# A block-matching convolution pipeline on one core: the first image's load and first strips, and the last image's transfers, put in another order and on other queues

## The chip, the cores and the metric

The kernel runs on one core of one Trainium2 chip. The time is the device time of one execution in microseconds (us); the figure for a kernel is the median of its runs. A profile was taken of one execution as well: it lists every instruction of the five engines (PE for matrix products, DVE, ACT, POOL, and SP, which only issues transfers) and the packets of the DMA queues.

## The reference, cut to what matters

The input is eight images of 32 channels and 128 x 128 pixels in f32. Two layers, each with a residual sum, are applied to them; each begins with a normalisation over groups of two channels of an image.

```python
# layer 0, on the normalised image x
for dy in range(-2, 3):
    for dx in range(-2, 3):
        sh = shifted copy of x (clipped at the edge)
        cost = 3x3 box sum of ((x - sh) ** 2).sum(channels)
idx = the 8 cheapest of the 25 offsets, for every pixel
g   = the 8 shifted copies that idx names          # 32 * 8 = 256 channels
h   = relu   (depthwise3x3(conv1x1(g, w1), w2))
h   = relu   (depthwise3x3(conv1x1(h, w3), w4))
h   = sigmoid(depthwise3x3(conv1x1(h, w5), w6))
y   = agg(inverse_dct(h * dct(g)));  x1 = x_in + y
# layer 1, on the normalised x1
out = x1 + conv(x1, one 5x5 kernel for every channel, padding 2)
```

## The kernel before, in words

**Steps.** An image is cut into 16 strips of 8 rows, with one more step after them for the rows that lag behind. The main loop (L1015) goes over all strips of all images, and in each step it works on three strips at once: stage 3 of strip s-2, stage 2 of strip s-1, stage 1 of strip s, then the end of strip s-2 (`for i in (3, 2, 1, 0)`, L1026). A stage is a 1x1 product (`pv` L641 and `p` L665), and a depthwise 3x3, half of it on DVE (`acc`, L692 to L699) and half on PE (`pw`, L718).

**Units.** The strip that enters next is gathered in four units, a half strip of four rows and half of the eight copies each. A unit has a load (`gather_load`: POOL fetches the pixels `xt`, L559/L565, and the indices `ib`, L574), a selection (`gather_select`: ACT turns indices into 0/1 masks `sel`, L588/L589), and the gathering itself (`gather_pixels`: PE multiplies pixels with masks, `pg` L603, and ACT copies the result to `xb`, L610). One unit is gathered in each part of a step.

**Preparation.** Before strips of an image can be gathered, its best offsets must be known. `prep` loads the image in four row groups of 32 rows with three rows around each (L84, and L89 for edge rows), takes statistics (L348), normalises (L359), then for six bands of rows subtracts shifted copies (`df`, DVE L413), squares them (ACT L421) and sums over channels (`pd`, PE L428). `costs` sums patches (`v`, L477 to L489; its input comes over two transfers through memory, L443 and L461/L468), transposes (`ct` L494/L498) and picks the eight cheapest offsets (DVE L505/L506, 32 pairs of instructions per row and group); `places` turns them into indices (`oc` L520 to L529, `pi` L538, `li` L540, stored by L541). This is done in four chunks of 8 rows in each of the four row groups, so strip n needs chunk n % 4, and the strips 0 to 3 need all four chunks.

**What sets the order.** PE, DVE and ACT execute in the order in which the program is written (`manual_schedule`, L999); POOL and SP are ordered by a scheduler. Preparation is cut into tasks that wait in queues D (DVE work, with a cost), A, P and Q. `tick` (L984) lets so much D work into each part of a step as the image's share asks for; `until` (L991) runs tasks until a condition holds; `push` takes a third value, a number of turns to wait. The 36 pairs of squares have cost `PAIR` = 1.95 and come first, in the order of the queue. A `unit` load first calls `until` the chunk that it needs is ready (L967 to L969), with everything written in between.

**The head.** The setup (L147 to L189) loads the depthwise weights (L122, L153), the three 1x1 weights (L173) and the dct weights (32 small transfers, L283) on the SP queue; the 1x1 weights are transposed on PE (L188) and copied by ACT (L189). The first image comes over the ACT queue alone. The loop L1005 loads units 0 to 6, for which chunk 1 must be ready, and gathers units 0 to 3. Then the steps begin.

**The tail.** Layer 1 of the last image runs after the last step. `load` (L840) reads four times 8 channels (L852, L854, L857), DVE normalises (L864), PE forms the 5x5 product by bands (L891), DVE adds it (L903) and the result goes out: for each group of 8 channels two halves e = 0, 1 of four channels, each in two transfers of the rows 0 to 61 and 66 to 127 (L905). The four rows between are computed apart (`middle`, L926 to L939, out at L948). All of these transfers are issued by POOL.

Of the kernel before, what the change touches and what calls it, by code (L numbers as in the profile page):

```python
# [19 lines left out]
R = 8  # L20
# [22 lines left out]
def bm3d_conv_preact(  # L43
# [33 lines left out]
    def load_image(b, engine):  # L77

        xn = xnp.tile([P, HR, HX], F32, name=f"xn_{b}", tag="xn")
        for rg in range(4):  # L80
            s = slice(C * rg, C * (rg + 1))
            lo = 32 * rg - 3
            a, z = max(lo, 0), min(lo + HR, H)
            engine.dma_start(xn[s, a - lo : z - lo, 2 : 2 + W], x[b, :, a:z, :])  # L84
            for r in range(HR):
                y = lo + r
                if y < 0 or y >= H:
                    y = min(max(y, 0), H - 1)
                    engine.dma_start(  # L89
                        xn[s, r : r + 1, 2 : 2 + W], x[b, :, y : y + 1, :]  # L90
                    )
        return xn

    first = load_image(0, nc.scalar)
# [52 lines left out]
    with tc.tile_pool(name="setup", bufs=1) as sp, tc.tile_pool(  # L147
        name="setup_ps", bufs=2, space=bass.MemoryType.PSUM
    ) as spp:
        dwt = sp.tile([P, 3, 4, 9], F32, name="dwt")  # L150
        for n, w in enumerate((w2, w4, w6)):
            for g in range(4):
                nc.sync.dma_start(  # L153
                    dwt[C * g : C * (g + 1), n],
                    w[:P].rearrange("(q c) o a b -> c q (o a b)", c=C),
                )
            nc.gpsimd.memset(dwd[0:C, n, 1], 0.0)
            for u in range(2):
                for dy in range(3):
                    s = slice(C * (u + dy), C * (u + dy + 1))  # L160
                    nc.gpsimd.tensor_tensor(
                        dwd[s, n, u],
                        cst[s, C_M32 : C_M32 + C]
                        .unsqueeze(1)
                        .unsqueeze(1)
                        .to_broadcast([C, 4, 3, C]),
                        dwt[s, n, :, 3 * dy : 3 * dy + 3].unsqueeze(3).to_broadcast([C, 4, 3, C]),
                        ALU.mult,
                    )
        wide = {}  # L170
        for name, w in (("w1", w1), ("w3", w3), ("w5", w5)):
            t = sp.tile([P, 2, CK], F32, name=f"nat_{name}", tag=f"nat_{name}")
            nc.sync.dma_start(t, w.rearrange("(m p) i a b -> p m (i a b)", p=P))  # L173
            if name == "w1":

                nat, t = t, sp.tile([P, 2, CK], F32, name="w1_kc")
                for m in range(2):
                    nc.vector.tensor_copy(
                        t[:, m].rearrange("p (k c) -> p k c", c=C),
                        nat[:, m].rearrange("p (c k) -> p k c", k=K),  # L180
                    )
            wide[name] = t
        for name, dst in (("w1", lw1), ("w3", lw3), ("w5", lw5)):
            for g in range(2):
                ps = spp.tile([P, CK], F32, name=f"ps_{name}_{g}", tag="ps")
                for m in range(2):
                    src = wide[name][:, m, g * P : (g + 1) * P]
                    nc.tensor.transpose(ps[:, m * P : (m + 1) * P], src, ident)  # L188
                nc.scalar.copy(dst[:, g], ps)  # L189
# [32 lines left out]
    def run(which, credit=1e9):  # L222

        q, took = queues[which], 0.0
        for _ in range(len(q) if which != "D" else 1000):
# [8 lines left out]
            )  # L234
            if i is None or took >= credit:
                break
# [37 lines left out]

    def mixes():
# [9 lines left out]
        yield "D", 1.0  # L285
# [529 lines left out]
    def layer1(b):  # L815
# [17 lines left out]
        last = b == NB - 1  # L833
        if last:
# [5 lines left out]
        def load(c):  # L840
# [11 lines left out]
            nc.gpsimd.dma_start(t[0], src[:, c : c + 4])  # L852
            for h in range(2):
                nc.gpsimd.dma_start(  # L854
                    t[1][64 * h : 64 * h + 64], src[64 - 64 * h : P - 64 * h, c + 4 : c + 8]
                )
            nc.gpsimd.dma_start(t[2], src[:, c + 4 : c + 8])  # L857
# [18 lines left out]
        for c in range(0, C, 8):  # L876
# [24 lines left out]
            for e in range(2):  # L901
                y = t[2 * e]
                nc.vector.tensor_add(y, y, ps[e])  # L903
                for a, z in ((0, 62), (66, P)):
                    nc.gpsimd.dma_start(  # L905
# [84 lines left out]

    def until(cond, credit):  # L991
        while not cond():
            now[0] += 1
            run("D", credit)
            run("A")
            run("P")
            run("Q")

    with tc.manual_schedule(engines=ORDERED):  # L999
        push(prep(0))  # L1000
        push(mixes())
# [3 lines left out]
        for u in range(7):  # L1005
            unit(gather_load, u)
            unit(gather_select, u - 2)
            unit(gather_pixels, u - 3)
        u = 4
# [5 lines left out]
        for s in range(len(steps) + 2):  # L1015
            if s < len(steps):
# [6 lines left out]
                if n == NS - 1 and b + 1 < NB:  # L1023
                    until(lambda: b + 1 in ready, 4.0)
                    xbd[b + 1] = dram.tile([P, 2, H, W], F32, name=f"xbd_{b+1}", tag="xbd")
            for i in (3, 2, 1, 0):  # L1026
# [21 lines left out]
                run("Q")  # L1048
                if s < len(steps):
                    unit(gather_select, u + 1, (0,))  # L1050
                    unit(gather_load, u + 3)
# [6 lines left out]
                if s < len(steps):  # L1058
# [4 lines left out]
                if s < len(steps):  # L1063
                    unit(gather_select, u + 1, (1,))
                    u += 1
                next(dt, None)
# [71 lines left out]
```

## Time and profile before

| | us |
|---|---|
| median of 4 runs | 6864.76 |
| the runs | 6874.87, 6871.53, 6846.25, 6857.99 |
| the profiled execution, own time | 6841.15 |
| its span, first to last instruction | 6839.4 |

| engine | busy, us | share of the span |
|---|---|---|
| PE | 6359.8 | 93% |
| DVE | 5856.3 | 86% |
| ACT | 5064.6 | 74% |
| POOL | 3241.2 | 47% |

| place in the span, us | what |
|---|---|
| 40.75 | statistics of the first image begin (L348) |
| 52.78 | first `df` (L413) |
| 137.66, 182.0, 230.19, 266.28 | indices of chunks 0 to 3 stored (L541) |
| 231.61, 271.45, 314.33, 357.15 | first product of strips 0 to 3 (L641) |
| 6779.56 | last rows of x1 of the last image have landed |
| 6796.21 | first result transfer issued (L905) |

The profile's page gives busy times for the whole span, the span in 40 slices, the DMA queues, the chain of work that ended last, and the costliest groups of instructions. Windows give the same busy times for chosen stretches; a timeline lists an engine's instructions with the idle time before them and what ended it. The view of DMA gives, for 40 slices of a stretch, the tenths of the time that the 16 engines were busy, and what each queue moved.

### The profile page before, as it was taken

How to read it: one execution, taken by the hardware profiler on the slowest of the kernel's cores; microseconds unless marked ns; L12 is line 12 of the kernel's file. 1: busy time of each engine (PE TensorE's matmuls, PEld its weight loads, DVE VectorE, ACT ScalarE, POOL GpSimd, SP SyncE). 2: the span in 40 equal slices, each digit the busy share in tenths (PEclk: the TensorE clock that was granted, in tenths of full speed). 3: DMA queues.
4: the chain of work that ended last, by engine and by line, in shares of the span. 5: the costliest groups of instructions: out<-in, count | busy, mean ns of one | idle time of the engine just before them, and what ended most of it. 6: DMA issues, size and time to landing. Idle time of an engine off the chain costs nothing.

```text
span 6839.4 us, 232443 instructions
## 1 busy us (share of the span) xinstructions
PE 6359.8 (93%) x101090; PEld 2969.0 (43%) x101090; DVE 5856.3 (86%) x8822; ACT 5064.6 (74%) x6698; POOL 3241.2 (47%) x5351
## 2 busy tenths in 40 slices
PE   4699899999999999999999999999999999999997
PEld 1344444444444444444444444444444444444443
DVE  6799988988888898888989888899888999877776
ACT  4687768777787777977778777787768777686772
POOL 6345436544464443644446444464435543344334
PEclk8899999999999999999999999999999999999998
DMA  3556656666566675665756657566565666566553
GB/s 80 135 150 149 155 135 159 162 147 161 148 154 156 150 162 142 165 148 146 171 130 163 161 144 168 133 169 155 149 153 150 166 157 147 139 163 159 149 151 82
DMA packets 809531, 1019.84 MB, mean 149 GB/s; under 512 B 255456, under 2 KB 619936, under 8 KB 808512
## 3 DMA queue, kind: packets, MB, share of 16 engines
q0 software_dynamic: 422432, 745.61, 42.5%
q1 hardware_dynamic: 381056, 256.86, 17.0%
q8 instruction: 796, 13.04, 0.8%
q10 hardware_dynamic: 5024, 2.49, 0.2%
q14 instruction: 223, 1.83, 0.1%
HBM read 553.25 MB, written 217.01 MB: 113 GB/s over the span
## 4 chain that ended last, share of the span: by engine, by line
PE 46%; DVE 14%; DMA 8%; ACT 6%; issue 5%; POOL 3%; SPq 0%; POOLq 0%; ACTq 0%; DVEq 0%
PE pw L718 16%; PE pv L641 11%; DVE acc L695 10%; PE p L665 10%; DMA t<-t 4%; PE pg L603 3%; PE p L891 2%; PE pc L777 2%; ACT ib L588 1%; PE pa L798 1%; PE pd L428 1%; ACT df L421 1%; DVE acc L785 1%; DMA ib<-idxd 1%; ACT acc L692 1%
## 5 line engine op out<-in xcount | busy, mean ns | idle before, releaser
L695 DVE SCALAR_TENSOR_TENSOR acc<-tv,dwv,acc 128x1024 f32<-128x1024 f32 (+3 forms) x3264 | 4032.3, 1237 | 255.3 <-ACT acc L692 139.0
L718 PE MATMUL pw<-t,dwd 96*32 96x508 f32 (+6 forms) x19392 | 2154.3, 591 | 125.2 <-DMA t<-t 101.3
L574 POOL DMA_DIRECT2D ib<-idxd x1024 | 569.8, 558 | 1827.3 <-ACT sel L589 1663.6
L718 PEld LDWEIGHTS pw<-t,dwd 96*32 96x32 f32 (+1 forms) x19392 | 712.6, 112 | 1248.2 <-issue 1153.9
L588 ACT ACTIVATE ib<-ib,nplace 128x1024 bf16<-128x1024 bf16 x1024 | 1170.2, 1143 | 18.5 <-DMA ib<-idxd 18.5
L589 ACT ACTIVATE sel<-ib 128x1024 f32<-128x1024 bf16 x1024 | 1084.7, 1059 | 32.5
L665 PE MATMUL p<-acc,lw 128*32 128x256 f32 x16768 | 994.0, 382 | 23.2 <-ACT tv L649 22.7
L641 PE MATMUL pv<-acc,lw 128*128 128x512 f32 (+1 forms) x2112 | 970.9, 601 | 28.6 <-DVE acc L785 20.0
L758 POOL DMA_DIRECT2D xf<-xbd x1088 | 651.5, 632 | 307.4 <-PE pc L777 80.9
L665 PEld LDWEIGHTS p<-acc,lw 128*32 128x32 f32 x16768 | 557.5, 111 | 452.8 <-ACT tv L649 62.4
L649 ACT COPY tv<-pv 128x512 f32<-128x512 f32 (+2 forms) x784 | 439.0, 577 | 400.7 <-PE pv L641 389.5
L603 PEld LDWEIGHTS pg<-sel,xt 128*32 128x32 f32 x45056 | 577.4, 111 | 265.8 <-ACT sel L589 66.4
L421 ACT ACTIVATE df<-df 128x786 f32<-128x786 f32 (+2 forms) x576 | 468.4, 859 | 297.1 <-DVE df L413 294.2
L603 PE MATMUL pg<-sel,xt 128*32 128x48 f32 x45056 | 595.5, 207 | 94.8 <-ACT sel L589 57.9
L731 ACT ACTIVATE acc<-pw 128x512 f32<-128x512 f32 (+2 forms) x808 | 441.6, 572 | 286.4 <-PE pw L718 286.0
L641 PEld LDWEIGHTS pv<-acc,lw 128*128 128x128 f32 x2112 | 379.3, 190 | 521.7 <-issue 399.1
L413 DVE TENSOR_TENSOR df<-xn 128x786 f32<-128x786 f32 (+2 forms) x576 | 527.5, 966 | 82.6 <-PE pd L428 81.8
L699 ACT ACTIVATE acc<-acc 128x1024 f32<-128x1024 f32 (+3 forms) x408 | 416.8, 1022 | 227.3 <-DVE acc L695 227.1
L672 ACT COPY t<-p 128x512 f32<-128x512 f32 x800 | 424.1, 570 | 128.0 <-PE p L665 125.9
L692 ACT ACTIVATE acc<-tv,dwv 128x1024 f32<-128x1024 f32 (+3 forms) x408 | 454.6, 1114 | 57.7 <-PE pa L798 39.8
L641 PE MATMUL pv<-xb,lw 128*128 128x512 f32 x1024 | 474.9, 606 | 0.0
L665 PE MATMUL p<-xb,lw 128*32 128x256 f32 x8192 | 467.7, 380 | 0.2 <-DVE xy L903 0.2
(151 smaller groups left out, 5774.8 us busy)
## 6 DMA issues: line engine op xcount, KB each, us to landing
ib<-idxd POOLq DMA_DIRECT2D x1024, 256.0 KB, 4.5
xbd<-xb POOLq DMA_DIRECT2D x128, 1024.0 KB, 7.0
xf<-xbd POOLq DMA_DIRECT2D x960, 128.0 KB, 7.0
t<-t SPq DMA_DIRECT2D x792, 128.0 KB
t<-t SPq DMA_DIRECT2D x384, 256.0 KB
tv<-tv SPq DMA_DIRECT2D x384, 130.0 KB
xt<-xtd POOLq DMA_DIRECT2D x240, 176.0 KB, 4.6
xl<-xs POOLq DMA_DIRECT2D x256, 64.0 KB, 2.7
```

The costliest lines, as they stand in the source:

```text
L413: nc.vector.tensor_sub(df[:, :, ca:cz], xn[:, r0 : r0 + SR, ca:cz], xn[:, r0 + dy : r0 + dy + SR, ca + dx : cz + dx],)
L421: nc.scalar.activation(df[:, :, ca:cz], df[:, :, ca:cz], AF.Square)
L574: nc.gpsimd.dma_start(ib.rearrange("p k y x -> p (k y x)"), idxd[b][s4 // 8, s4 % 8, 4 * k0 : 4 * k0 + 8] .rearrange("k x -> (k x)") .part ...
L588: nc.scalar.activation(ib, ib, AF.Square, bias=nplace)
L589: nc.scalar.activation(sel, ib, AF.Relu, scale=-1.0, bias=1.0)
L603: nc.tensor.matmul(pg[C * j : C * (j + 1), :, xa:xz], xt[:, t], sels[j // 2][:, j % 2, :, xa:xz], start=True, stop=True,)
L641: nc.tensor.matmul(ps[:, :hr], lhsT[:, g, P:CK], src(g)[:, h : h + hr], start=g == 0, stop=g == 1,)
L665: nc.tensor.matmul(ps[C * r : C * (r + 1), e, :nb], lhsT[:, g, s], rows[:, r : r + 4 * nb - 3 : 4], start=g == 0, stop=g == 1,)
L692: nc.scalar.activation(acc, rows, AF.Copy, scale=tap)
L695: nc.vector.scalar_tensor_tensor(acc, rows, tap, acc, op0=ALU.mult, op1=ALU.add)
L718: nc.tensor.matmul(pt[u][C * j : C * (j + 1), : nh[u], :nb, xa:xz], dwd[0:hi, i - 1, u, j, dx + 1], t[0:hi, j, : nh[u], :nb, xa + dx : xz ...
L758: nc.gpsimd.dma_start(xf[p : p + C, m, j0:j1], src[g, m, (h + m + 1) % 2, :, :, ya:yz])
```

## The change

The first image's four row groups are issued in turn by ACT (groups 0 and 2) and SP (1 and 3), ahead of the constants `cst` on SP. The transposition of the 1x1 weights is no longer part of the setup: it is a task, `weights`, which is due after 8 turns, takes its tiles from the accumulators' places and its PSUM from `ps_x`; the mixing weights (`mixes`) are due after 10 turns. While chunk 0 isn't ready, `run` takes D tasks that aren't squares first. The main loop's beginning is written anew: only units 0 to 3 are gathered ahead of it; in steps 0 to 3 the units of the next strip are begun by `begin` (three loads, three turns of tasks, a selection) and gathered in groups by `whole` (selection, load, a turn, gathering), in the counts of `count`, and no unit behind `limit` is loaded, so that a step no longer asks for a later chunk than its own units need. From step 4 on the loop is as before. In the last image, `queue` puts the loads and the results of the half e = 0 on SP and those of e = 1 on ACT (L852 and L857 on SP, L854 on ACT); the four rows of `middle` stay on POOL.

```diff
@@ -74,10 +74,11 @@
         tc.tile_pool(name="ps_d", bufs=1, space=bass.MemoryType.PSUM)
     )
 
-    def load_image(b, engine):
+    def load_image(b, *engines):
 
         xn = xnp.tile([P, HR, HX], F32, name=f"xn_{b}", tag="xn")
         for rg in range(4):
+            engine = engines[rg % len(engines)]
             s = slice(C * rg, C * (rg + 1))
             lo = 32 * rg - 3
             a, z = max(lo, 0), min(lo + HR, H)
@@ -91,7 +92,7 @@
                     )
         return xn
 
-    first = load_image(0, nc.scalar)
+    first = load_image(0, nc.scalar, nc.sync)
     cst = const.tile([P, C_N], F32, name="cst")
     nc.sync.dma_start(cst, consts)
     ident = cst[:, C_ID : C_ID + P]
@@ -144,9 +145,7 @@
     nc.vector.tensor_scalar(inner, inner, -1.0, 1.0, op0=ALU.mult, op1=ALU.add)
 
 
-    with tc.tile_pool(name="setup", bufs=1) as sp, tc.tile_pool(
-        name="setup_ps", bufs=2, space=bass.MemoryType.PSUM
-    ) as spp:
+    with tc.tile_pool(name="setup", bufs=1) as sp:
         dwt = sp.tile([P, 3, 4, 9], F32, name="dwt")
         for n, w in enumerate((w2, w4, w6)):
             for g in range(4):
@@ -167,26 +166,6 @@
                         dwt[s, n, :, 3 * dy : 3 * dy + 3].unsqueeze(3).to_broadcast([C, 4, 3, C]),
                         ALU.mult,
                     )
-        wide = {}
-        for name, w in (("w1", w1), ("w3", w3), ("w5", w5)):
-            t = sp.tile([P, 2, CK], F32, name=f"nat_{name}", tag=f"nat_{name}")
-            nc.sync.dma_start(t, w.rearrange("(m p) i a b -> p m (i a b)", p=P))
-            if name == "w1":
-
-                nat, t = t, sp.tile([P, 2, CK], F32, name="w1_kc")
-                for m in range(2):
-                    nc.vector.tensor_copy(
-                        t[:, m].rearrange("p (k c) -> p k c", c=C),
-                        nat[:, m].rearrange("p (c k) -> p k c", k=K),
-                    )
-            wide[name] = t
-        for name, dst in (("w1", lw1), ("w3", lw3), ("w5", lw5)):
-            for g in range(2):
-                ps = spp.tile([P, CK], F32, name=f"ps_{name}_{g}", tag="ps")
-                for m in range(2):
-                    src = wide[name][:, m, g * P : (g + 1) * P]
-                    nc.tensor.transpose(ps[:, m * P : (m + 1) * P], src, ident)
-                nc.scalar.copy(dst[:, g], ps)
 
     xbp = ctx.enter_context(tc.tile_pool(name="xb", bufs=2))
     accp = ctx.enter_context(tc.tile_pool(name="acc", bufs=1))
@@ -232,6 +211,9 @@
                 ),
                 None,
             )
+            if which == "D" and 0 not in ready:
+
+                i = next((k for k, (c, _, at) in enumerate(q) if at <= now[0] and c != PAIR), i)
             if i is None or took >= credit:
                 break
             cost, task, _ = q[i]
@@ -272,6 +254,35 @@
         yield from inverse_std(mr[:, 1:2], tmp[:, 0:1], tmp[:, 0:1])
         return mr
 
+    def weights():
+
+        natural, kc = {}, None
+        for i, (name, w) in enumerate((("w1", w1), ("w3", w3), ("w5", w5))):
+            t = accp.tile([P, 2, R * W // 2], F32, name=f"nat_{name}", tag=f"acc{i + 1}0")
+            natural[name] = t = t[:, :, :CK]
+            nc.sync.dma_start(t, w.rearrange("(m p) i a b -> p m (i a b)", p=P))
+        yield "D", 1.0, 8
+
+        nat = natural["w1"]
+        kc = accp.tile([P, 2, R * W // 2], F32, name="w1_kc", tag="acc31")
+        natural["w1"] = kc = kc[:, :, :CK]
+        for m in range(2):
+            nc.vector.tensor_copy(
+                kc[:, m].rearrange("p (k c) -> p k c", c=C),
+                nat[:, m].rearrange("p (c k) -> p k c", k=K),
+            )
+        for name, dst in (("w1", lw1), ("w3", lw3), ("w5", lw5)):
+            for g in range(2):
+                yield "P", 0
+                ps = ps_x.tile([P, 512], F32, name=f"ps_{name}_{g}", tag="x")
+                for m in range(2):
+                    nc.tensor.transpose(
+                        ps[:, m * P : (m + 1) * P],
+                        natural[name][:, m, g * P : (g + 1) * P],
+                        ident,
+                    )
+                nc.scalar.copy(dst[:, g], ps[:, :CK])
+
     def mixes():
 
         dq = work.tile([P, 2, K], F32, name="dq", tag="dq", bufs=1)
@@ -282,7 +293,7 @@
                     p = 64 * h + 8 * k
                     nc.sync.dma_start(dq[p : p + 8, m], src[m, (h + m + 1) % 2, k])
         m8 = work.tile([P, 8], F32, name="m8", tag="m16", bufs=1)
-        yield "D", 1.0
+        yield "D", 1.0, 10
         nc.vector.tensor_reduce(
             m8,
             cst[:, C_M32 : C_M32 + C].rearrange("p (a c) -> p c a", c=8),
@@ -831,6 +842,7 @@
         bc = work.tile([P, 2, C], F32, name=f"bc_{b}", tag="bc")
         nc.scalar.copy(bc.rearrange("p a b -> p (a b)"), pb[:, : 2 * C])
         last = b == NB - 1
+        queue = [nc.sync, nc.scalar] if last else [nc.gpsimd] * 2
         if last:
             ends = xnp.tile([P, HR, HX], F32, name="ends", tag="xn")
             ends = ends.rearrange("p r x -> p (r x)")[:, : 8 * 4 * W]
@@ -849,12 +861,12 @@
                     for name, e in (("xy", 0), ("xm", 0), ("xy", 1), ("xm", 1))
                 ]
             src = x1d[b].rearrange("c y x -> y c x")
-            nc.gpsimd.dma_start(t[0], src[:, c : c + 4])
+            queue[0].dma_start(t[0], src[:, c : c + 4])
             for h in range(2):
-                nc.gpsimd.dma_start(
+                queue[1].dma_start(
                     t[1][64 * h : 64 * h + 64], src[64 - 64 * h : P - 64 * h, c + 4 : c + 8]
                 )
-            nc.gpsimd.dma_start(t[2], src[:, c + 4 : c + 8])
+            queue[0].dma_start(t[2], src[:, c + 4 : c + 8])
             xys[c] = t
 
         def normalise(c):
@@ -902,7 +914,7 @@
                 y = t[2 * e]
                 nc.vector.tensor_add(y, y, ps[e])
                 for a, z in ((0, 62), (66, P)):
-                    nc.gpsimd.dma_start(
+                    queue[e].dma_start(
                         out[b, c + 4 * e : c + 4 * e + 4, a:z].rearrange("c y x -> y c x"),
                         y[a:z],
                     )
@@ -988,25 +1000,46 @@
         owed[0] -= run("D", owed[0]) if owed[0] > 0 else 0
         owed[0] = min(owed[0], 6.0)
 
+    def turn(credit=4.0):
+        now[0] += 1
+        run("D", credit)
+        run("A")
+        run("P")
+        run("Q")
+
     def until(cond, credit):
         while not cond():
-            now[0] += 1
-            run("D", credit)
-            run("A")
-            run("P")
-            run("Q")
+            turn(credit)
 
     with tc.manual_schedule(engines=ORDERED):
         push(prep(0))
+        push(weights())
         push(mixes())
         xbd[0] = dram.tile([P, 2, H, W], F32, name="xbd_0", tag="xbd")
         for i in range(3):
             nc.gpsimd.memset(tb[i][0:64, :, 0], 0.0)
-        for u in range(7):
-            unit(gather_load, u)
-            unit(gather_select, u - 2)
-            unit(gather_pixels, u - 3)
-        u = 4
+
+        def begin(u):
+            for k in range(3):
+                unit(gather_load, u + k)
+
+            for _ in range(3):
+                turn()
+            unit(gather_select, u)
+
+        def whole(u, end):
+            if u + 1 < end:
+                unit(gather_select, u + 1)
+            if u + 3 < end:
+                unit(gather_load, u + 3)
+            turn()
+            unit(gather_pixels, u)
+            return u + 1
+
+        begin(0)
+        u = 0
+        while u < 4:
+            u = whole(u, 4)
 
         dt = dv = kept = iter(())
 
@@ -1023,6 +1056,12 @@
                 if n == NS - 1 and b + 1 < NB:
                     until(lambda: b + 1 in ready, 4.0)
                     xbd[b + 1] = dram.tile([P, 2, H, W], F32, name=f"xbd_{b+1}", tag="xbd")
+
+            count = {0: (0, 0, 0, 0), 1: (2, 2, 0, 0), 2: (2, 2, 0, 0), 3: (2, 2, 2, 2)}
+            count = count.get(s, (1, 1, 1, 1)) if s < len(steps) else (0, 0, 0, 0)
+            limit = 4 * (s + 1) if s < 3 else len(units)
+            if 0 < s < 4:
+                begin(u)
             for i in (3, 2, 1, 0):
                 si = s - (i - 1 if i else 2)
                 live = 0 <= si < len(steps)
@@ -1046,23 +1085,30 @@
                     final_dct(bi, ni, accs[3, bi, ni], xf, j0, j1)
 
                 run("Q")
+                more = count[3 - i]
+                if more:
+                    if u + 1 < limit:
+                        unit(gather_select, u + 1, (0,))
+                    if u + 3 < limit:
+                        unit(gather_load, u + 3)
                 if s < len(steps):
-                    unit(gather_select, u + 1, (0,))
-                    unit(gather_load, u + 3)
                     tick(b, i)
                 next(later, None)
                 next(new_v, None)
                 if live and i:
                     pointwise_t(i, bi, ni, lws[i - 1], src)
                 next(kept, None)
-                if s < len(steps):
+                if more:
                     unit(gather_pixels, u)
                 next(dt, None)
                 run("A")
                 next(dv, None)
-                if s < len(steps):
-                    unit(gather_select, u + 1, (1,))
+                if more:
+                    if u + 1 < limit:
+                        unit(gather_select, u + 1, (1,))
                     u += 1
+                    if more > 1:
+                        u = whole(u, limit)
                 next(dt, None)
                 kept, dv, dt = dv, new_v, new_t
                 if live and not i:
```

## The prediction

> **What bounds the kernel now.** I read the page first: the span in 40 slices, with PE's granted clock below.
>
> ```profile
> PE   4699899999999999999999999999999999999997
> ...
> PEclk8899999999999999999999999999999999999998
> ```
>
> PE is full from the third slice (171 us each) to the last but one. The change leaves this middle alone: in the lists of instructions by engine, PE, DVE and ACT have the same order in both kernels from the third-stage product `pv` of strip 2 (379 us) to the last image's transfers. So only the head, up to that product, and the tail, from the last x1 rows (6779.56 us), can change. I read the head in windows of 50 us: busy time of PE, PEld, DVE, ACT and POOL, then clock, DMA share and GB/s.
>
> ```profile
> 0.00:50.00 50.00, 5.79 (x22) 4.24 (x22) 11.16 (x27) 6.15 (x17) 27.02 (x43) 1.00 0.44 77
> ...
> 150.00:200.00 50.00, 22.31 (x398) 11.05 (x398) 26.94 (x115) 25.16 (x31) 18.44 (x31) 0.57 0.25 58
> ...
> 250.00:300.00 50.00, 42.82 (x735) 20.72 (x731) 44.17 (x138) 37.28 (x48) 14.60 (x24) 0.95 0.68 169
> 300.00:350.00 50.00, 50.00 (x878) 25.13 (x868) 39.79 (x36) 42.47 (x55) 15.17 (x27) 1.00 0.61 154
> ```
>
> PE has work for 50 of 50 us only from 300 us on; before that it waits. For what, the timeline of ACT (issues, start and length in us) and the waits of the first 300 us tell (total, times, longest):
>
> ```profile
> 0.75 0.42 ACTq L84 DMA_DIRECT2D xn<-in_x_dram  x1
> ...
> 11.35 19.36 ACTq L84 DMA_DIRECT2D xn<-in_x_dram  x3
> 37.06 1.80 ACTq L89 DMA_DIRECT2D xn<-in_x_dram  x3
> 38.88 1.28 ACT L189 ACT_TABLE_LOAD   x1 [38.88 <-DMA xn<-in_x_dram]
> ```
>
> ```profile
> DVE mx L505 <- ACT ct L498: 39.3, 3, 24.8
> ACT L189 <- DMA xn<-in_x_dram: 38.9, 1, 38.9
> PE pi L538 <- DVE oc L529: 36.3, 4, 20.2
> ```
>
> One big load is issued in 0.42 us, yet three take 19.36: they wait for earlier transfers. The image is in at 36 us; PE's `pi` and DVE's top-k stand behind squares that are written ahead of them. The tail I read in the chain that ended last (start, length) and in DMA's issues (KB each, us to landing).
>
> ```profile
> 6799.27 6.02 POOL out_dram L905 x4
> ...
> 6809.93 1.50 POOL out_dram L905
> 6811.43 16.86 DMA out_dram<-xo
> ```
>
> ```profile
> ends<-x1d POOLq DMA_DIRECT2D x4, 256.0 KB, 3.9
> ...
> out_dram<-ends POOLq DMA_DIRECT2D x8, 124.0 KB, 12.4
> out_dram<-xo POOLq DMA_DIRECT2D x8, 124.0 KB, 14.8
> ```
>
> POOL issues 16 results at 1.5 us each, 24 us; DVE has the last one ready at 6815.2, POOL issues it by 6822.5. And a result of 124 KB takes three times as long as a load of 256 KB: 127 KB / 12.4 us = 10 GB/s against 262 / 3.9 = 67. Its packet records show two shares of 31 rows each (62 = 2 x 31), where transfers of 32 or 128 rows show 16. Keep this for below.
>
> **Head, step by step.** (1) *Load.* In the new list none of the image's transfers on ACT waits, nor the two big ones on SP. The four big loads are then queued at once: 4864 packets of 512 B (2.49 MB) at 44 ns each (22.6% of 16 engines x 60 us / 5024 packets = 43), over 16 engines, 13.5 us; image in at 15 to 16, not 36. `cst` comes after it on SP (0.41 us of issue), then 12 `dwt` at 0.71 (8.5 us), three weights, 32 `dq` at 0.8 (25.5), all on SP, now until 54 instead of 40. The weights' transposes (8 on PE, 4.1 us of ACT with its copies) no longer stand before the statistics; later, they cost PE nothing, which is idle (5.8 of 50 us busy), and are in (3) for ACT. Statistics 15.5 to 21.3 (4.84 + 0.37), group statistics as before 4.2, normalise 2.9, first `df` at 28.5 instead of 52.78: gain 24.
>
> Here a rule of the Trainium skill speaks against the change. The row first: three loads by one queue took 19.36 us of ACT where one took 0.42. "DMA: Bandwidth & Descriptors", section "Issuing engines are not separate DMA queues", says that transfers of all issuers run on the same 16 DMA engines, and that several issuers only save issuing time, which is usually small. By the rule the load gains some 2 us and the head comes to nothing or a loss; by the row, where issuing waits, it gains 20. The run decides; no row contradicts the rule's first half.
>
> (2) *First chunk.* POOL's depthwise weights (L161, 17 us) now run beside the first `df` and may hold DVE (4.22 to 6.5 shows four DVE instructions that all ended when POOL's memsets did): 0 to 4, I take 2. DVE's `ldct` and `ib` are due after 10 turns and meet `dq` that lands at 52: 2.5 to 4 us of wait, with the squares queued behind it. The sums of chunk 0 start at 78 instead of 95.58: gain 17.6. The wait from the last `sm` to them (17.4) stays.
>
> (3) *Chunks.* DVE's order is new: top-k (four pairs of L505/L506 in 1.66) goes before squares until chunk 0 is done. `oc` of chunk 0 ends at about 106 (134.5 before). ACT then makes chunk 0's masks (2.14 a pair, 9 us) among squares, which costs DVE 8 us of waiting in the ring of four `df`. Chunk 1: about 170 (180.9); chunk 2: 210 (229); then DVE waits some 10 us for `tv`, as ACT has masks ahead of it. Before chunk 3 the new order also puts two groups of eight `acc` (10.3 each) and the 5x5 bands (7): chunk 3 ends at 269 instead of 265.2. That is where most of the early gain is given back.
>
> (4) *From `pi` of chunk 3 to the meeting point*, PE had 114 us before. Of this work 32 is now done earlier (in the idle time at clock 0.57); 82 is left: 5 pairs of `pv` and `p` (7.2), 11 `pg` (1.0), 6 `pw` (5.2), 4 for the end of a strip. But ACT has 100 us of its own from 252 on (26 mask pairs, copies, first taps), so it runs out at about 353, and PE follows 9 to 13 behind: 362 to 366 against 379. **Head: -16**, from 0 (ACT and DVE waits double) to -30 (PE's 82 us hold unhindered).
>
> **Tail.** Loads are issued 8 us sooner on two queues, but ACT's come behind its copy of `bc` (6782.1), so the second half's normalisation is 1 us later; PE follows; the last add stays near 6815. POOL's 24 us of issuing are replaced by 0.4 to 0.8 each on SP and ACT (L84, `dq`), 6 at most on each, beside DVE. Nothing is queued on either behind the results. What is late next are the transfers. 16 x 124 KB = 2.03 MB, cut in two shares of 31 rows each.
> - Time of one engine for one MB: 72 us on SP (17.0% of 16 x 6839.4 / 256.86 MB), 81 for POOL's results (480 packets of 4096 B, 333 ns mean), 87 on ACT's load; at the best rate shown, 290 GB/s on 16 engines, 55.
> - How many engines take part: POOL's are spread (33% of 16 = 5 at a time). On SP and ACT no row shows a transfer in two shares. Ends: all shares on one pair of engines, or spread over all.
>
> One pair: 1.016 MB x 78 (between SP's row for the packets and POOL's for the write) = 79; 6796.2 + 79 + 2.1 (last data to the end of the span now) = 6877.5: **+38**, from +15 (55) to +47 (87). Spread: last issue at 6817, 10 to 12 us to land, the middle rows out by then: -10. The break-even is where 2.03 x 78 / n fits in the 41 us from 6796.2 to 6837.3: n = 3.9 engines. I take one pair: POOL writes each transfer by a program, at 1.5 us, and can place it anew; SP and ACT issue a load of any size in 0.4, which looks like a fixed scheme. This is a judgement.
>
> The same page, section "Why a DMA increments its semaphore by 16 and not by 1", says that a transfer uses the largest number up to 16 that divides its slowest dimension, and that from SP and ACT these are always the lowest-numbered engines, from POOL a run that moves on. For 62 rows that is engines 0 and 1 each time; the sum by the rule is +38, without it anything from -10. The two shares of POOL's records agree with the first half; no run here shows the second yet.
>
> **Sum.** -16 + 38 = +22 on the profiled execution (6841.15, which is 23.6 below the median of the runs): 6863 there, 6864.76 + 22 = **6887** on the median.
>
> **Rivals.**
> - *Head as above, results spread* (the faster side): -16 - 10 = -26, 6839. For it: POOL's same transfers are spread. Against: each issue by POOL is another kind. Decides from 3.9 engines for the tail, from 4.4 (36 us) for a gain over 0.3%.
> - *One pair, head given back*: chunk 3's `oc`, already later in my walk, comes another 15 us later, as DVE's idle time (31 to 39 of 50 us busy) is ordered waits and not slack: head 0 to +5, net +41, 6906. That the load isn't faster, since both queues' transfers wait as ACT's did, ends there too: 20 of the 24 are lost.
> - *Both*, head nothing and results spread: -10, 6855.
>
> **How the numbers follow.** Chances: forecast 0.55, spread 0.25, head given back 0.15, both 0.05. 0.3% (20.6 us) is about what a measurement here can tell from no change. The forecast's own range is -15 to +47 with both terms at an end, in most cases 0 to +45: 0.33 slower, 0.20 same, 0.02 faster. Spread: 0.22 faster, 0.03 same. Head given back: 0.15 slower. Both: 0.05 same. Faster 0.24, same 0.28, slower 0.48. The range runs from the spread case (6839, with a little below it) to the last but the worst of the third: 6836 to 6915.
>
> **What would show it.** Load: the last image row lands at 15 to 16, first `df` at 28 (else step 1 fails). `oc` of chunk 0 near 106, of chunk 3 near 269; the product `pv` of stage 3, strip 2, near 364. Tail: DMA share near 2/16 with 25 to 30 GB/s from 6796 shifted on, results landing after 30 us and more, the chain's last link a long result transfer; if the share is 4/16 or above, the pair is wrong. The whole fails if the middle isn't the same, which PE's slices would show.

## The result, and the profile after

The changed kernel takes 6872.87 us (median of 35 runs, 6847.77 to 6888.2) against 6864.53 (57 runs, 6846.25 to 6898.32): ratio 1.0012, 95% interval 1.0006 to 1.0019. It is slower by some 8 us, less than the 20.6 that the prediction called "same". The profiled execution took 6877.73 us, with a span of 6876.0.

That span is 36.6 us longer than the one profiled before, and most of this is not the change. I cut both spans at two marks: the third-stage product `pv` of strip 2, from which on the order is the same, and the issue of the last x1 rows.

| stretch, us | before | after |
|---|---|---|
| head: to the product of stage 3, strip 2 | 378.64 | 378.59 |
| middle, the same instructions in both | 6397.6 | 6425.9 |
| tail: from the issue of the last x1 rows to the end | 63.14 | 71.51 |

The middle differs between executions of any of the kernels below: the profiles have it between 6397 and 6436 us. The tail's +8.4 and the head's 0 agree with the 8.3 between the medians. From here on I therefore compare the two marks of each profile, and ratios where several runs were made.

The head first, in the same windows (PE, PEld, DVE, ACT, POOL busy; clock, DMA share, GB/s).

```profile
0.00:50.00 50.00, 18.08 (x78) 5.47 (x78) 29.96 (x39) 17.50 (x26) 37.59 (x47) 1.00 0.52 85
...
150.00:200.00 50.00, 26.09 (x244) 10.29 (x246) 43.14 (x171) 15.15 (x24) 18.08 (x31) 0.72 0.32 90
...
250.00:300.00 50.00, 36.88 (x534) 16.97 (x538) 36.91 (x139) 27.93 (x37) 9.48 (x16) 0.79 0.31 72
300.00:350.00 50.00, 45.92 (x763) 21.93 (x756) 34.83 (x33) 37.39 (x47) 15.19 (x27) 0.97 0.54 142
```

The first 50 us hold 18 us of PE work instead of 6: the head starts earlier. But from 250 to 350 us PE is busy for 82.8 us where it was for 92.8. The gain is there, and is given back. The load, in the timelines of ACT and DVE:

```profile
0.76 0.43 ACTq L85 DMA_DIRECT2D xn<-in_x_dram  x1
1.22 1.84 ACTq L90 DMA_DIRECT2D xn<-in_x_dram  x3
3.08 0.45 ACTq L85 DMA_DIRECT2D xn<-in_x_dram  x1
```

```profile
30.42 15.10 DVE L424 TENSOR_TENSOR df<-xn 128x792 f32<-128x792 f32 x12
```

None of the four big image loads waits any more (of the rows at the image's edge, the three that SP issues still take 8.63 us together), and the first `df` is at 30.42 us (52.78 before). The indices of the four chunks (`pi`, PE) come at 107.3, 170.9, 210.6 and 286.1 us, where they came at 134.6, 180.9, 229.2 and 265.2. So chunk 0 is 27 us early, and chunk 3 is 21 us late. PE's timeline shows a hole just ahead of chunk 3 (start, length, what; in brackets the idle time before it and what ended it):

```profile
232.60 3.66 PE L676 MATMUL p<-xb,lw 128*32 128x256 f32 x64
250.98 8.59 PE L729 MATMUL pw<-t,dwd 96*32 96x512 f32 x48 [14.71 <-issue]
...
286.08 0.66 PE L549 MATMUL pi<-cst,oc 128*128 128x128 f32 x2 [12.14 <-DVE oc L540]
```

"issue" is time for which the view names no releaser. The wait that PE's queue executes there (16.1 us, begun at 234.8) stands ahead of the products that need the rows `t<-t`, which SP issues from 236.94 to 239.5, and POOL issues half of the second image beside them:

```profile
237.43 1.70 POOL L85 DMA_DIRECT2D xn<-in_x_dram  x2 [0.17 <-issue]
```

Now the tail. The view of DMA for 6775 to 6876 us shows tenths of 16 engines and GB/s in slices of 2.5 us, ACT's timeline the issues.

```profile
DMA  4610021350001499997001111111121111111110
GB/s 116 149 53 3 20 58 27 86 135 13 0 6 23 130 291 221 211 257 136 0 17 42 43 43 43 44 43 43 44 66 43 44 43 43 43 43 43 43 44 17
```

```profile
6810.11 10.02 ACTq L866 DMA_DIRECT2D ends<-x1d  x8
6825.85 39.22 ACTq L917 DMA_DIRECT2D out_dram<-xo  x8
```

The loads ran at 211 to 291 GB/s, on all engines or nearly all; the results run at 43 GB/s, at a share of 14% of the 16 engines, for 48 us. The packets of the two queues (SP's is q1, ACT's q10; packets, MB, share) from 6830 to 6870 us, and then from 6872.9 to 6873.9 us, when SP's results are through:

```profile
q10 hardware_dynamic: 1706, 0.87, 7.2%
q1 hardware_dynamic: 1690, 0.86, 7.1%
```

```profile
DMA packets 85, 0.04 MB, mean 44 GB/s; under 512 B 0, under 2 KB 85, under 8 KB 85
...
q10 hardware_dynamic: 85, 0.04, 14.3%
```

Alone, ACT's queue has the rate and the share that both had together. So both were held by the same engines, as the case of one pair said. That these are two is not named in any view; I take it from 62 = 2 x 31 rows and from the share (14.3% of 16 is 2.3 at a time, with packets that overlap). They are much faster than I took: 2.03 MB in 48 us is 21 GB/s for each, 47 us for an MB.

### The profile page after: what moved, and what is told of

It is laid out like the page before. It is cut to its first block, busy times and chain, and to the rows that moved or that the text cites. A ratio compares the mean times of both kernels' runs of the same rounds, so it can differ in the third digit from the quotient of the medians.

```text
span 6876.0 us, 232445 instructions
## 1 busy us (share of the span) xinstructions
PE 6373.7 (93%) x101090; PEld 2963.8 (43%) x101090; DVE 5856.3 (85%) x8822; ACT 5066.2 (74%) x6698; POOL 3214.4 (47%) x5319
## 4 chain that ended last, share of the span: by engine, by line
PE 55%; DVE 20%; ACT 9%; DMA 8%; issue 5%; POOL 3%; SPq 0%; ACTq 0%; POOLq 0%; DVEq 0%
PE pw L729 19%; PE pv L652 13%; DVE acc L706 13%; PE p L676 11%; DMA t<-t 4%; PE pg L614 4%; PE p L903 2%; PE pc L788 2%; ACT ib L599 2%; DVE df L424 2%; ACT df L432 2%; DVE idx L517 1%; PE pa L809 1%; PE pd L439 1%; DVE acc L796 1%
```

## The experiments

The theory after the result: the tail's +8 comes from two DMA engines carrying all results. The head's early gain is lost by chunk 3, in part in the 14.7 us for which PE waits for rows that lie among the second image's load. Rivals: the writes themselves are slow; the head's loss lies in the order of instructions alone, or the head really is faster and the profile caught a bad execution.

| run | head mark | tail | ratio to before, interval |
|---|---|---|---|
| changed kernel | 378.6 | 71.5 | 1.0012 (1.0006 to 1.0019) |
| head_alone | 377.1 | 65.1 | 0.9997 (0.9986 to 1.0007) |
| tail_alone | 379.6 | 71.7 | 1.0010 (0.9999 to 1.0021) |
| results_split | 377.0 | 52.3 | 0.9986 (0.9977 to 0.9994) |
| second_load_later | 370.6 | 72.3 | 1.0003 (0.9992 to 1.0014) |
| load_alone | 362.9 | 71.8 | 0.9998 (0.9989 to 1.0007) |
| one_queue | 390.2 | 74.1 | 1.0039 (1.0026 to 1.0052) |
| later_and_split | 373.5 | 55.3 | 0.9975 (0.9962 to 0.9989) |
| before_split | 379.9 | 48.1 | 0.9975 (0.9964 to 0.9985) |
| joined | 362.4 | 50.6 | 0.9957 (0.9943 to 0.9970) |
| squares_first | 358.1 | 72.3 | one execution |
| bands_later | 379.3 | 71.8 | one execution |
| results_on_pool | 379.1 | 65.8 | one execution |

The head mark is the start of the third-stage product of strip 2 in us from the start of the span; where the timeline joins it with its neighbours I took it from the second image's first product on PE, which stands 12.5 us behind it in every kernel.

### head_alone

```diff
-        queue = [nc.sync, nc.scalar] if last else [nc.gpsimd] * 2
+        queue = [nc.gpsimd] * 2
```

> The changed kernel with all transfers of the last image's 5x5 product back on POOL, so the new head alone. Theory (the head's earlier chunks are lost again in one wait of PE for transfers at 236 to 251 us, the tail's pair of engines costs the 8 us): third-stage product of strip 2 at 378 to 379 us as in both kernels, tail of 63 us from the issue of the last x1 rows to the end, ratio to the kernel before 0.9995 to 1.0005. Rival (the head does gain, and the one profile caught a bad execution): product at 362 to 368, ratio 0.9977.

Head 377.1, ratio 0.9997: the new head is worth nothing; the interval leaves it 0.14% at most. The rival's 0.9977 is outside the interval.

### tail_alone

In the kernel before:

```diff
+        queue = [nc.sync, nc.scalar] if last else [nc.gpsimd] * 2
-            nc.gpsimd.dma_start(t[0], ...)
+            queue[0].dma_start(t[0], ...)
...
-                    nc.gpsimd.dma_start(
+                    queue[e].dma_start(
```

> The kernel before with only the last image's transfers on SP and ACT. Theory: results go out at 43 GB/s, tail of 71 to 72 us instead of 63, ratio to the kernel before 1.0012. Rival (the tail is worth nothing, the 8 us come from the middle): tail of 63, ratio 1.000.

Tail 71.7, as in the changed kernel. The ratio's interval just holds 1, so it is the mark that carries this: 8.5 us more than before in the tail.

### results_split

```diff
-                for a, z in ((0, 62), (66, P)):
+                for a, z in ((0, 48), (48, 62), (66, 114), (114, P)) if last else ((0, 62), (66, P)):
```

> The changed kernel with each result transfer of 62 rows of the last image cut into 48 and 14 rows, the same bytes and queues. Theory (62 rows go over two DMA engines, the same two each time; 48 and 14 rows go over 16 and 14): the last result lands within 6 us of its issue, tail of 50 to 53 us, 19 to 21 less than the changed kernel, ratio to the kernel before 0.998. Rival (writing these rows is what is slow, whoever carries them): the rate stays near 43 GB/s and the tail near 71, or longer by the 16 more issues.

The same bytes, by the same two queues, in twice as many transfers, and the tail is 19.2 us shorter than the changed kernel's. The DMA view of its last 36 us:

```profile
DMA  9500279404893000005970000038931000000000
GB/s 209 116 5 0 71 159 236 116 0 106 163 210 86 0 0 0 0 0 141 207 211 6 0 0 0 0 97 169 242 76 37 18 0 0 0 0 0 0 0 0
```

Bursts of 160 to 240 GB/s and pauses have taken the place of the flat 43. The rival, that writing these rows is slow, is out: it was the cut in two shares.

### second_load_later

```diff
             for i in (3, 2, 1, 0):
+                if s == 3:
+                    if i == 3:
+                        second.append(xnp.tile([P, HR, HX], F32, name="xn_1", tag="xn"))
+                    rg = 3 - i
+                    rows = slice(C * rg, C * (rg + 1))
+                    nc.scalar.copy(second[0][rows, 3, 2:3], cst[rows, C_Q : C_Q + 1])
+                    load_rows(1, rg, second[0], nc.gpsimd)
...
```

The rest of the edit takes `load_rows` out of `load_image` and hands this tile to `prep`. The six edge rows (16 KB each) are not held back.

> The changed kernel with the load of the second image held back: each of its four row groups waits for one ACT copy of 32 elements in the four parts of step 3. Theory (PE's 14.7 us wait at 236 us is for row transfers that lie among 1.2 MB of the second image and index loads): the wait is gone or below 4 us, indices of chunk 3 ready at 274 instead of 286, third-stage product of strip 2 at 365 to 369 instead of 378.6, ratio to the kernel before 0.9994 (head -12, tail +8). Rival (the order of the instructions makes the wait, the transfers are only beside it): chunk 3 at 286 and the product at 378, ratio 1.0012.

Half right. PE's timeline:

```profile
243.00 7.10 PE L734 MATMUL pw<-t,dwd 96*32 96x512 f32 x48 [7.45 <-DMA t<-t]
...
276.62 0.66 PE L554 MATMUL pi<-cst,oc 128*128 128x128 f32 x2 [12.14 <-DVE oc L545]
```

The wait is 7.45 us instead of 14.71, and now the view names the rows as its releaser. Chunk 3 is 9.5 earlier and the head 8.0 shorter. So the second image's load is worth some 8 us, and as much wait again has another cause; the index loads (five of 256 KB) and the copy of `xb` (1 MB) are still beside the rows. I didn't separate these.

### load_alone and one_queue

In load_alone the changed kernel has the start of the kernel before, in the loop of the steps too:

```diff
-        begin(0)
-        u = 0
-        while u < 4:
-            u = whole(u, 4)
+        for u in range(7):
+            unit(gather_load, u)
+            unit(gather_select, u - 2)
+            unit(gather_pixels, u - 3)
+        u = 4
...
-            if which == "D" and 0 not in ready:
-                i = next(...)
```

> The changed kernel with the start of the kernel before: seven units loaded ahead of step 0, chunk 2 asked for in step 0, one unit in each part, squares first; what stays of the change is the load over two queues, the weights as a task, and the tail. Theory (the 20 us of the load are real, and it is the order of the new start that gives them back, partly by the second image's load in the way of PE's row transfers): third-stage product of strip 2 at 356 to 364 us, tail 71, ratio to the kernel before 0.9985 to 0.9995. Rival (whatever comes early in the head meets the same wait for transfers): product at 374 to 380, ratio 1.000 to 1.0012.

In one_queue:

```diff
-    first = load_image(0, nc.scalar, nc.sync)
+    first = load_image(0, nc.scalar)
```

> The changed kernel with all of the first image's load on ACT's queue again. Theory: first df 15 to 20 us later (at 46 to 50), each chunk as much later, no overlap of PE's row transfers with the second image's load or one at another place, third-stage product of strip 2 at 388 to 398, ratio to the kernel before 1.0025 to 1.004. Rival (the load's time doesn't reach the end of the head): product at 376 to 382, ratio 1.0012.

With the old start, the fast load (and the weights as a task) brings the head to 362.9: 15.7 less than before. With the new start and the slow load it ends at 390.2. So the load's time does reach the end of the head, in both orders (15.7 and 11.6 us), and the new start costs 15.7 over the old one. The ratio of load_alone is 0.9998, where I had 0.9985 to 0.9995; the marks give (-15.7 + 8.7) / 6864 = -0.1%, which its interval just holds. In one_queue PE's wait ahead of `pw` is 14.77 us, as in the changed kernel: it moves with the whole head, since the second load follows the first image's squares.

### later_and_split and before_split

> The changed kernel with the second image's load held back and the results cut into 48 and 14 rows. Theory (head and tail add up): third-stage product of strip 2 at 370, 8 less than before, tail 52, 11 less than before; ratio to the kernel before 0.9972. Rival (a part of either is noise): 0.9985 or more.

> The kernel before with each result transfer of the last image cut into 48 and 14 rows, still issued by POOL. Theory (POOL's 1.5 us for 62 rows is the price of many descriptors on two engines; the 64-row load costs 0.63): 32 issues at 0.4 to 0.65, some 17 us instead of 24, landing within 4 us, tail 53 to 57 us instead of 63, ratio to the kernel before 0.9988. Rival (an issue costs 1.5 us whatever its rows): 48 us of issuing, tail 80 or more, ratio 1.0025.

later_and_split has both edits above in one kernel. Each mark is some 3 us above the one expected; together they give 0.9981, which the interval of the ratio holds, so head and tail add up. before_split is the kernel before with the cut of results_split, on POOL. Its tail is 15 us shorter, 5 to 9 more than expected. POOL's timeline has the price of an issue:

```profile
6819.80 2.35 POOL L905 DMA_DIRECT2D out_dram<-ends  x4 [6.99 <-DVE ends L903]
6822.14 2.30 POOL L905 DMA_DIRECT2D out_dram<-xo  x4
```

0.58 us for one, so 1.16 for the 62 rows that cost 1.52 uncut; and the last of them is issued 4.3 us after the last add, where it was 7.3 (6815.2 to 6822.5). Another 3.9 us of the 15 are a shorter DRAIN of POOL at the end of the program, shown with joined below. The tail that the change moved off POOL had its best remedy in the rows, and none in the queues.

### squares_first, bands_later, results_on_pool and joined

In squares_first:

```diff
-            if which == "D" and 0 not in ready:
-                i = next((k for k, (c, _, at) in enumerate(q) if at <= now[0] and c != PAIR), i)
```

> The changed kernel without the rule that D takes other tasks ahead of squares until chunk 0 is ready. Theory (the rule brings chunk 0 forward and chunk 3 back, and chunk 3 is what the head ends on): indices of chunk 0 at 118 to 122 instead of 107, chunk 3 no later than 286, third-stage product of strip 2 at 374 to 380. Rival (the rule is what loses 16 us against the old start): product at 363 to 366.

Here my theory fell, and the rival's 363 to 366 was too high as well. Without this one rule the head ends at 358.1: better than with the old start, and 20.5 us better than the changed kernel. (It is one execution, but four profiles with the changed head have its mark at 377.0 to 379.1.) PE's timeline shows the last two chunks:

```profile
190.91 0.44 PE L546 MATMUL pi<-cst,oc 128*128 128x128 f32 x2 [3.01 <-DVE oc L537]
...
232.83 0.66 PE L546 MATMUL pi<-cst,oc 128*128 128x128 f32 x2 [15.63 <-DVE oc L537]
```

Chunk 0 comes 11 us later (118.5), and then chunks 1, 2 and 3 come 15, 20 and 53 us earlier. From 100 to 290 us, PE waits 29.3 us for squares in the changed kernel and 17.7 without the rule, DVE 29.3 and 16.4 for `ct`. Without the rule the second image's load is issued from 176 to 223 us, ahead of strip 1's rows, and PE doesn't wait at their product `pw`.

In bands_later:

```diff
-                if s == 2:
+                if s == 5:
                     push(bands())
```

> The changed kernel with the preparation of the 5x5 bands put off from step 2 to step 5. Theory (DVE makes them ahead of chunk 3's top-k while PE waits for it): indices of chunk 3 at 276 to 280 instead of 286, third-stage product of strip 2 at 369 to 373 instead of 378.6. Rival (ACT and PE behind chunk 3 are the bound): chunk 3 earlier, product at 376 or later.

Chunk 3 comes at 275.0, 11 us earlier, and the head ends where it did (379.3). PE's timeline shows why:

```profile
274.99 0.69 PE L549 MATMUL pi<-cst,oc 128*128 128x128 f32 x2 [11.02 <-DVE oc L540]
275.48 5.47 PE L652 MATMUL pv<-acc,lw 128*128 128x512 f32 x8
280.87 3.66 PE L676 MATMUL p<-acc,lw 128*32 128x256 f32 x64
```

The products `pv` and `p` that stood ahead of `pi` in the changed kernel (265.84 to 273.0 us) now stand behind it, and PE waits 11.02 us for chunk 3 where it waited 12.14. So the head doesn't end on chunk 3's time but on how long PE stands idle. The windows from 0 to the head mark say the same (us):

| run | head mark | PE busy | PE idle |
|---|---|---|---|
| before | 378.64 | 229.57 | 149.1 |
| changed kernel | 378.59 | 235.36 | 143.2 |
| squares_first | 358.08 | 232.78 | 125.3 |
| bands_later | 379.33 | 233.25 | 146.1 |

The windows count 3270 or 3271 products of PE in each. The changed head has 5.8 us less of idle time than before, and loses it again as its products take 5.8 us longer. The mean granted clock of its window is 0.82, 0.86 before; but load_alone has 0.82 as well and 232.9 us busy, so what makes them longer isn't shown.

In results_on_pool:

```diff
-                    queue[e].dma_start(
+                    nc.gpsimd.dma_start(
```

> The changed kernel with the last image's results on POOL again, uncut, and only its loads on SP and ACT. Theory (the loads on ACT, behind the copy of the means, cost 3 to 5 us, the two engines the rest): tail 65 to 68 us. Rival (the loads gain what the change meant them to): tail 55 to 62.

65.8, as the theory had it: the loads on two queues gain nothing against head_alone's 65.1. They cost less than the 3 to 5 us of the theory: 0.7 against head_alone, 2.7 against the kernel before. The second half's normalisation waits 5.0 us for ACT's loads (5.6 in the changed kernel).

> The better part of each run so far: load over two queues with the weights as a task, the start of the kernel before, the last image's loads on POOL, its results cut into 48 and 14 rows on SP and ACT. Theory (head and tail add up): third-stage product of strip 2 at 363 (16 less than before), tail 45 to 48 us (15 to 18 less), ratio to the kernel before 0.9953. Rival (less time in the head comes back as waits in the steps that follow): 0.998.

joined is load_alone with the last image's loads on POOL and the cut results on SP and ACT: 0.9957, the fastest of all runs, as the marks add up (-16.3 and -12.6 give 0.9958). Its tail is 3 to 6 us above what I expected: the last packet is through at 6822, and the span ends at 6830.2. What stands there is a DRAIN of POOL behind its last issue, at the end of the program (number, then the shortest, median and longest in ns, then the first and last start in us):

```profile
L1147 POOLq DRAIN  x3: 46/98/9032, 6820.4 to 6829.9; - x3
```

Every kernel here has it: 9.0 us in joined, 6.6 in results_on_pool, 3.9 in before_split, 7.6 to 7.9 in all others. In the changed kernel it is over 18 us before the slow results are through and costs nothing; in the kernel before, and with cut results, the span ends on it. What it waits for isn't shown. The start of squares_first with this tail should be 4 us better still; that wasn't run.

## Why the prediction was right or wrong

The time fell in the range (6836 to 6915), on the forecast's side, but well below the forecast of 6887: two terms were wrong, and their errors partly cancel, which is luck. Predicted: head -16, tail +38, sum +22. Measured: head 0, tail +8.4, and 8.3 between the medians.

- **What bounds the kernel.** Right: only head and tail changed, and PE's middle is the same work.
- **Load (1).** Right: image in at 17 us (15 to 16 said), first `df` at 30.4 (28.5), and 17.8 us of it are due to the two queues alone (48.26 in one_queue). The rule of the Trainium skill that was set against it ("DMA: Bandwidth & Descriptors", section "Issuing engines are not separate DMA queues": several issuers only save issuing time) would have given some 2 us; here the issues themselves waited for earlier transfers, so the time saved was not small.
- **First chunk (2)** and the first three chunks of **(3).** Right: sums at 79.1 (78), chunks at 107, 171 and 211 (106, 170, 210). While POOL built the depthwise weights, 12 `df` took 1.26 us each, afterwards 0.90: the 2 us taken were 4.
- **Chunk 3 in (3).** This is the step of the head that failed: 286 where I had 269. I missed the wait for row transfers beside the second image's load. The prediction looked at the queues that the first image's load moved past, and not at what the freed `xn` lets POOL load next, 1.2 MB at a time. And I put what is given back down to two groups of `acc` and the bands; bands_later shows that the bands cost the head nothing. The rule that puts squares off was priced at 8 us of DVE's waiting; it costs the head 20.5 us (squares_first). Some 8 of them go when the second image's load is held back (second_load_later); how the rest divides among the waits isn't shown.
- **From chunk 3 to the meeting point (4).** 92.5 us, 95 said, but the agreement says little. The distance was 113.4 before, 104.3 in bands_later and 125.3 in squares_first, so it can't be added to whatever time chunk 3 has: in bands_later chunk 3 came at 275, near the 269 forecast, and the head still ended at 379.
- **Tail, one pair or spread.** Right: one pair, by the flat 43 GB/s and by results_split. The section "Why a DMA increments its semaphore by 16 and not by 1" of the same page (the largest number up to 16 that divides the rows, on SP and ACT the lowest-numbered engines) agrees with the runs: 62 rows crawl, 48 and 14 don't, and both queues share the 43 GB/s. Which engines they are no view names.
- **Tail, time of one engine for one MB.** This term was mis-sized: 78 us taken, 55 as the lower end, 47 measured. I read the time that packets took among others as the engine's capacity. In the tail the same 512 bytes took 27 ns a packet, and an engine finished one in 24, so packets overlap. With full queues and nothing beside them these two reached 21 GB/s each, where the best row before had 290 GB/s on 16, 18 each.
- **Tail, loads.** Said: 1 us later by ACT's place behind the means. Measured: DVE waits 5.6 us for them, and the last add is 1.7 us later. (What ACT loads are the swapped rows of the second half, L854; the rows of both halves to which the results are added come over SP.)
- **Rivals.** "One pair, head given back" is the case that happened, with chance 0.15; I gave its price as +41, of which 30 was the tail's wrong size. The mechanism given there (chunk 3 another 15 us late, as DVE's idle time is ordered waits) was right in size, 17; but it named neither the rule for squares nor the second image's load, to which the runs put it down.

By parts, added in this order, the change is now: fast load with the weights put off -15.7, new start without the rule -4.8, the rule +20.5, last image's transfers +8.4.

## What to carry to other kernels

Count the rows of a transfer before moving it to another queue: 62 rows crawled at 43 GB/s, and cutting them into 48 and 14 was worth more (15 to 19 us) than any choice of queue. When a head is made to start earlier, follow each chunk to the last one: bringing the first chunk forward by 11 us put the last one back by 53. And when a buffer comes free at another time, ask what load that triggers, and whose small transfers it will stand among.

## What the runs showed of the hardware that was not expected

- The results of 62 rows, in 512-byte packets, went out at 43 GB/s from two queues together, and at the same rate from one alone (21 GB/s for each of two engines), without a break for 48 us; before, POOL's same rows went at 51 GB/s on average over the tail, at a share of 33% of the engines.
- POOL needs 1.52 us to issue 62 rows of 2 KB and 1.16 us for the same rows as 48 and 14.
- POOL's DRAIN at the end of the program took 7.6 to 7.9 us in eleven of the fourteen kernels, 3.9 to 9.0 in the others. With cut results on SP and ACT the span therefore ended 7.0 and 8.3 us after the last packet (results_split, joined), with the uncut ones 1.2 (the changed kernel), with cut ones on POOL 2.6 (before_split).
- The same middle of the same order took 6397 to 6436 us in different executions, a spread of 39 us, more than all that the change does.
